# A selective scan and a soft mixture of experts over 16 sequences: four states by TensorE in three sequences, an expert group begun earlier, and a tail in another order

## The chip, the cores and the metric

The kernel is written for one core of a Trainium2 chip. A core has five engines with a queue of instructions each: TensorE (PE) for matrix products, VectorE (DVE), ScalarE (ACT) for functions from tables, GpSimd (POOL), and SyncE (SP), which here only issues DMAs. PSUM takes TensorE's results; the kernel counts it in eight banks, of which a product of 128 x 512 fills one. The metric is device time in microseconds (us) of the whole program. All data are fp32.

## The reference

The input is x of 16 sequences, 512 positions, 256 features. Two layers follow each other, and each adds its input and normalizes. Cut to what matters:

```python
# layer 1: a selective scan in both directions
xf, res = split(x @ in_proj.T)                     # 2 x 512 channels
xf = silu(causal_depthwise_conv(xf))               # again for the backward direction
dt, B, C = split(xf @ x_proj.T)                    # 16, 16 and 16 columns
dt = softplus(dt @ dt_proj.T + b)
dA = dt * A;  dB_u = dt * u * B                    # for each of 16 states
dA_cum = exp(reversed cumsum of shifted dA)
xs = cumsum(dB_u * dA_cum) / (dA_cum + 1e-12)
y = sum over states(xs * C) + u * D                # times silu(res); two directions added
x = layernorm(x + y @ out_proj.T)
# layer 2: soft experts
xn = layernorm(x) * g + b
logits = xn @ slot_embeds_normed                   # 16 experts x 64 slots
dispatch = softmax(logits, over positions)
combine  = softmax(logits, over slots)
slots = dispatch.T @ xn
eo = (gelu(slots @ Wg + bg) * (slots @ Wu + bu)) @ Wd + bd
x = layernorm(x + combine @ eo)
```

## The kernel before

Everything is in one function, `seq_layers`, which goes through the sequences b = 0 to 15. Channels lie on the partitions: 512 channels are four chunks of 128, and a chunk's 512 positions lie along the free axis.

**The scan** (`scan_part`, lines 392 to 470) is the spine. It is called four times for a sequence: for each of the two pairs of chunks (p = 0, 1), forward and then backward (r = 0, 1). Inside, the 16 states are taken in eight pairs n, n+1, and for each pair come the two chunks, so a sequence has 64 chunk steps. In each step POOL multiplies `db = du * bs` (line 427), where `bs` is a row of B broadcast to all partitions by a DMA; ACT makes the decay `exp(dt * A)` (line 444) and a tanh (446); DVE scans along the positions (450 forward, 452 backward) and gates the result, `hg` (455); POOL multiplies by the broadcast row of C, `cs` (456); and TensorE adds the products into an accumulator in PSUM through multiplications by an identity matrix (371).

For two of the 16 states POOL is spared: `DIAG = (5, 13)`, line 31. There `db` is half as long, and TensorE makes the other half: `du` transposed, times a matrix with B's row on its diagonal (`by_diagonal`, line 405), lands as `hd` in a bank of PSUM, and the scan reads it from there. The diagonal matrices lie in DRAM in `diag_dram` (86). They are zeroed once by DMAs on ACT's queue (187 and 188); in `project_unit` a DMA on ACT's queue writes the diagonal's elements, singly (297); and a DMA on SP's queue loads a state's matrices as `dg`, one state pair ahead of its use (420). `dg` has one buffer.

**Work beside the scan.** The rest is cut into pieces by Python generators, which `class Side` (472 to 534) lets in between chunk steps. There are three sides: `prep` prepares the projections of the next part of the scan, `front` finishes a sequence (`finish`, 613: out projection, layer norm, and `dispatch`, 680), and `back` has the experts and the combines. A piece that fills a bank of PSUM yields HOLD, until its result is taken a step later; a generator that waits yields WAIT; GAP asks for a step without a piece. The three sides share the banks that are free (`BANKS`). `begin(steps)` sets the pace: a side's planned pieces are spread over so many chunk steps. A side runs its generators one after another. Within an engine the order of instructions is the order in which this program issues them.

**Layer 2.** `dispatch` makes logits `pl` (687) in eight steps of 128 slots, the softmax over positions `et` on ACT (700), transposes it `pd` (704), and multiplies by the positions `pq` (719); the slots go to DRAM (`s_dram`, 738). `experts(g, lo, hi)` (740) takes two sequences at once, as group g: sequences 2g and 2g+1. It loads weights and slots (`st`, 763), and for each of eight pairs of experts computes `pg` (825, 830), gelu, `pu` (779), and `peo` (806), and writes to `e_dram` (868). `combine(b)` loads these results (`ceo`), makes the softmax over slots (`weights`, 875: logits `cl` 884, exponentials `cm` 898, transposes `ctp` 905), and multiplies: `cpo` (962).

**The main loop** (995 to 1024) adds at each odd b from 3 on the group of experts (b-3)/2 and its two combines to `back`, spread over 128 chunk steps, or 64 in the last sequence. So group 6 (sequences 12 and 13) starts with b = 15. After the last scan comes the **tail** (1025 to 1049), without a scan: `finish(15)` beside `all_weights(14)`, which makes combine weights ahead of time; when both have ended, `experts(7)` beside `all_weights(15)`; when both have ended, the two last combines.

The lines of the main loop and the tail that the change touches:

```python
if b >= 3 and b % 2 == 1:
    g = (b - 3) // 2
    back.add(8 * PAIR, experts(g, 0, 8))
...
back.begin(128 if b % 2 == 1 and b + 1 < nb else 64)
...
back.add(1, all_weights(2 * g, kept))
side_by_side()
front.add(1, experts(g, 0, 8))
back.add(1, all_weights(2 * g + 1, kept))
side_by_side()
```

Of the kernel before, what the change touches and what calls it, by code (L numbers as in the profile page):

```python
# [29 lines left out]
NE = 16  # L30
DIAG = (5, 13)
DIAG_SIZE = P * (P + 1)
# [23 lines left out]
def seq_layers(tc, ident, neghalf, a, out):  # L56
# [22 lines left out]
    with ExitStack() as ctx:  # L79
# [5 lines left out]

        diag_dram = drams.tile([2, len(DIAG), NL, DIAG_SIZE], F32, name="diag_dram")
        const = ctx.enter_context(tc.tile_pool(name="m_const", bufs=1))
# [86 lines left out]

        def constants():
            steps(side[0], "f", "")
            projections(side[1], "b", "_b")
            steps(side[1], "b", "_b")
            outT = const.tile([P, ND, DM], F32, name="outT")
            nc.sync.dma_start(outT, a["out_projT"].rearrange("(c p) o -> p c o", p=P))  # L180
            late(nc.vector.tensor_scalar(outT, outT, 0.5, None, ALU.mult))
            return outT
# [3 lines left out]
        nc.vector.memset(blank, 0.0)  # L186
        for part in diag_dram.rearrange("r i l (p s) -> (r i) p l s", p=P):
            nc.scalar.dma_start(part, blank[:, : NL * (P + 1)].rearrange("p (l s) -> p l s", l=NL))

# [73 lines left out]
        def prep_gate(b, fwd, out):  # L263
# [9 lines left out]
            out["res"] = res  # L273

        def project_unit(b, r, out):

            w = side[r]
            q = f"{b}_{r}"
            yield GAP + 1
            px = bank(f"px_{q}")  # L280
            for c in range(ND):
                nc.tensor.matmul(
                    px[:XW, :], w["xT"][:, c, :], out["u"][:, c, :], start=(c == 0), stop=(c == ND - 1)
                )
            yield HOLD
            xd = p1.tile([XW, L], F32, tag=f"xd_{r}", name=f"xd_{q}")
            bc = dram.tile([2, NS, L], F32, tag="bc", name=f"bc_{q}")
            if r == 0:
                late(nc.scalar.activation(xd, px[:XW, :], AF.Identity, bias=unit))
            else:  # L290

                late(nc.scalar.activation(xd[: XB + NS, :], px[: XB + NS, :], AF.Identity, bias=unit[: XB + NS]))
                nc.scalar.copy(xd[XC:XW, :], px[XC:XW, ::-1])
            nc.sync.dma_start(bc[0], xd[XB : XB + NS, :])
            nc.sync.dma_start(bc[1], xd[XC:XW, :])
            step = DIAG[1] - DIAG[0]
            nc.scalar.dma_start(
                diag_dram[r].rearrange("i l (p s) -> i l p s", p=P)[:, :, :, 0],
                xd[XB + DIAG[0] : XB + NS : step, :].rearrange("i (l p) -> i l p", p=P),
            )  # L300
            out.update(xd=xd, bc=bc)
# [90 lines left out]
        def scan_part(b, r, p, v, accs, done, then):  # L392

            prep.drain()
            prep.gens += [[1, g] for g in [turn_pair(b, r, p, v)] + then]
            w = side[r]
            made = {}
# [12 lines left out]
            for n in range(0, NS, 2):  # L410
                q = f"{b}_{r}_{p}_{n}"
                k = 1 if n + 1 in DIAG else 2

# [3 lines left out]
                nc.sync.dma_start(cs, v["bc"][1, n : n + 2, :].unsqueeze(0).to_broadcast([P, 2, L]))  # L417
                if n + 3 in DIAG:
                    dg = p4.tile([P, L], F32, tag="dg", name=f"dg_{q}", bufs=1)
                    nc.sync.dma_start(  # L420
                        dg.rearrange("p (l s) -> p l s", l=NL),
                        diag_dram[r, DIAG.index(n + 3), :, : P * P].rearrange("l (p s) -> p l s", p=P),
                    )
                for c in chunks:
# [37 lines left out]
                    nxt_n = n if c == chunks[0] else n + 2  # L462
                    if nxt_n + 1 in DIAG:
                        for x in sides:
                            x.take_up()
                        by_diagonal(nxt_n + 1, chunks[1] if c == chunks[0] else chunks[0])
# [146 lines left out]
        def finish(b, y):  # L613
# [64 lines left out]
            yield from dispatch(b, xn, x2T)  # L678

        def dispatch(b, xn, x2T):  # L680

            for sc in range(NSC):
# [30 lines left out]
                if sc % 2 == 1:  # L713
# [14 lines left out]
                    for k in range(NM):  # L728
# [7 lines left out]
                        if k == 0:  # L736
                            late(ins)
                    nc.scalar.dma_start(s_dram[b, :, :, h * 256 : (h + 1) * 256].rearrange("k p s -> p k s"), sl)

        def experts(g, lo, hi):  # L740
# [22 lines left out]
            def load_slots(ep):  # L763
# [6 lines left out]
                return st  # L770

            prefetch()
            st = load_slots(lo)
            yield 0
            def up(e, j, st):
                pu = bank(f"pu_{g}_{e}")
                for fc in range(NF):
                    for k in range(NM):
                        nc.tensor.matmul(  # L779
                            pu[:, fc * P : (fc + 1) * P],  # L780
                            got["Wu", e][:, k, fc * P : (fc + 1) * P],
                            st[:, k, :, j * SL : (j + 1) * SL],
                            start=(k == 0),
                            stop=(k == NM - 1),
                        )
                used[0] += 1
                return pu
# [28 lines left out]
            for ep in range(lo, hi):  # L816
                e0 = 2 * ep
                yield 2
                pgs = []
# [33 lines left out]
                pus = [up(e0 + j, j, st) for j in range(2)]  # L853
                if ep + 1 < hi:
                    st = load_slots(ep + 1)
                bd = p2.tile([P, 2, DM], F32, tag="bd", name=f"bd_{g}_{e0}", bufs=1)
# [10 lines left out]
                late(nc.vector.tensor_tensor(eo.rearrange("p e o -> p (e o)"), po, bd.rearrange("p e o -> p (e o)"), ALU.add))  # L867
                nc.sync.dma_start(e_dram[e0 : e0 + 2, b0 * SL : (b0 + 2) * SL, :].rearrange("e s o -> s e o"), eo)

        def load_x2(b, lc):  # L870
# [57 lines left out]
        def combine(b, kept=None):  # L928

            own = e_dram[:, b * SL : (b + 1) * SL, :].rearrange("(c j) s o -> j s c o", j=2)  # L930
            eos = []
# [13 lines left out]
            nc.sync.dma_start(x1, x1_dram[b].rearrange("(c p) d -> p c d", p=P))  # L945
            x2 = [] if kept else [load_x2(b, 0)]
            yield 0
# [8 lines left out]
            for lc in range(NL):  # L956
                i = f"{b}_{lc}"
                cts, sm = kept.pop((b, lc)) if kept else (yield from weights(b, lc, x2, False))
                yield GAP + 1
# [35 lines left out]
        for b in range(nb):  # L995
            bwd, nxt, accs = {}, {}, {}

            if b >= 3 and b % 2 == 1:
                g = (b - 3) // 2
                back.add(8 * PAIR, experts(g, 0, 8))  # L1000
# [3 lines left out]
            front.begin(64)  # L1004
            back.begin(128 if b % 2 == 1 and b + 1 < nb else 64)

# [34 lines left out]
        g, kept = nb // 2 - 1, {}  # L1041
        back.add(1, all_weights(2 * g, kept))
        side_by_side()
        front.add(1, experts(g, 0, 8))
        back.add(1, all_weights(2 * g + 1, kept))
        side_by_side()
        front.add(1, combine(2 * g, kept))
        back.add(1, combine(2 * g + 1, kept))
        side_by_side()
# [46 lines left out]
```

## Time and profile before

| what | value |
|---|---|
| time, three runs | 5405.57, 5410.14, 5413.56 us (median 5410.14) |
| the profiled execution | 5411.23 us, its span 5409.4 us |
| busy: POOL, DVE, PE, ACT | 87%, 84%, 80%, 76% of the span |
| weight loads of TensorE | 63%, beside its products |
| TensorE's granted clock, mean | 0.889 of full speed |
| DMA | 907.73 MB, 168 GB/s on average |

The costliest groups of instructions on the page, each with its line, engine, operation, output and inputs, shape, count, then busy time and mean ns of one, then the engine's idle time just ahead of them and what ended most of it:

```profile
L456 POOL TENSOR_TENSOR hg<-hg,cs 128x1024 f32<-128x1024 f32 x1024 | 2420.8, 2368 | 128.1 <-DVE hg L455 110.0
L427 POOL TENSOR_TENSOR db<-du,bs 128x1024 f32<-128x1024 f32 (+1 forms) x1024 | 2144.4, 2098 | 232.3 <-DVE h L450 84.7
L371 PE MATMUL acc<-ident,hg 128*128 128x128 f32 x8192 | 1179.3, 295 | 203.3 <-POOL hg L456 181.6
L455 DVE SCALAR_TENSOR_TENSOR hg<-th,h 128x512 f32<-128x512 f32 x1792 | 1185.8, 678 | 177.2 <-PE acc L371 90.4
L452 DVE TENSOR_TENSOR_SCAN h<-h,db 128x512 f32<-128x512 f32 x896 | 1072.8, 1218 | 112.2 <-ACT h L444 107.5
```

POOL's two multiplications make 4565 of its 4732 us. A share of the whole span is a mean over parts with different limits: the page's 40 slices of 135 us show POOL idle in the last two, where the tail has no scan, and TensorE at five or six tenths in the first seven, where there are no experts yet.

```profile
PE   5656666898888978788888977889787897888889
POOL 6999999999999899998999989998999989988600
```

### The profile page before, as it was taken

What the parts mean: (1) busy time and instruction counts of PE and PEld (TensorE: products, weight loads), DVE (VectorE), ACT (ScalarE), POOL (GpSimd) and SP (SyncE); (2) the same over time, 40 slices, a digit from 0 to 9 for tenths busy, and PEclk for the clock granted to TensorE, in tenths of its full rate; (3) what the DMA queues carried; (4) which work ended last, traced back from release to release, by engine and by line L of the source; (5) the groups of instructions that cost most, each with busy time, mean ns of one, the idle gap of its engine ahead of it and who ended that gap; (6) DMA issues with size and microseconds to landing.
All of it is one profiled execution on the core that took longest, in us unless ns stands there. A gap on an engine that the chain in (4) does not pass through costs nothing. (4 is left out here: it accounts for less than half of the span.)

```text
span 5409.4 us, 73721 instructions
## 1 busy us (share of the span) xinstructions
PE 4331.1 (80%) x24144; PEld 3390.0 (63%) x24145; DVE 4559.7 (84%) x6276; ACT 4087.2 (76%) x6515; POOL 4732.1 (87%) x2537
## 2 busy tenths in 40 slices
PE   5656666898888978788888977889787897888889
PEld 3445555676666666677656765667656776667657
DVE  7888988889898899888998888988899889988722
ACT  6677777787888778887877887788788887877641
POOL 6999999999999899998999989998999989988600
PEclk7778778898899988899888989899889998989999
DMA  4334333575446644566446754467444764457436
GB/s 137 131 117 137 125 129 131 189 230 159 156 142 212 225 149 148 158 223 213 131 144 194 232 170 153 132 212 232 149 149 146 225 224 134 145 179 234 126 103 188
DMA packets 595236, 907.73 MB, mean 168 GB/s; under 512 B 78082, under 2 KB 384898, under 8 KB 594852
## 3 DMA queue, kind: packets, MB, share of 16 engines
q1 hardware_dynamic: 521156, 859.87, 49.5%
q10 hardware_dynamic: 73696, 43.14, 2.8%
q8 instruction: 192, 3.15, 0.2%
q14 instruction: 192, 1.57, 0.1%
HBM read 840.86 MB, written 62.01 MB: 167 GB/s over the span
## 5 line engine op out<-in xcount | busy, mean ns | idle before, releaser
L456 POOL TENSOR_TENSOR hg<-hg,cs 128x1024 f32<-128x1024 f32 x1024 | 2420.8, 2368 | 128.1 <-DVE hg L455 110.0
L427 POOL TENSOR_TENSOR db<-du,bs 128x1024 f32<-128x1024 f32 (+1 forms) x1024 | 2144.4, 2098 | 232.3 <-DVE h L450 84.7
L371 PE MATMUL acc<-ident,hg 128*128 128x128 f32 x8192 | 1179.3, 295 | 203.3 <-POOL hg L456 181.6
L455 DVE SCALAR_TENSOR_TENSOR hg<-th,h 128x512 f32<-128x512 f32 x1792 | 1185.8, 678 | 177.2 <-PE acc L371 90.4
L371 PEld LDWEIGHTS acc<-ident,hg 128*128 128x128 f32 x8192 | 1044.9, 154 | 390.8 <-POOL hg L456 240.9
L452 DVE TENSOR_TENSOR_SCAN h<-h,db 128x512 f32<-128x512 f32 x896 | 1072.8, 1218 | 112.2 <-ACT h L444 107.5
L450 DVE TENSOR_TENSOR_SCAN h<-h,db 128x512 f32<-128x512 f32 x896 | 1071.1, 1217 | 48.8 <-ACT h L444 45.7
L446 ACT ACTIVATE th<-rr,Ah_f 128x512 f32<-128x512 f32 x1024 | 725.0, 714 | 186.3 <-DVE hg L455 183.1
L446 ACT ACTIVATE th<-rr,Ah_b 128x512 f32<-128x512 f32 x1024 | 721.5, 712 | 155.2 <-DVE hg L455 147.7
L444 ACT ACTIVATE h<-dt,A_f 128x512 f32<-128x512 f32 x896 | 608.2, 680 | 117.5 <-DVE hg L455 112.6
L444 ACT ACTIVATE h<-dt,A_b 128x512 f32<-128x512 f32 x896 | 608.6, 681 | 108.8 <-DVE hg L455 105.1
L687 PE MATMUL pl<-x2T,seT 128*128 128x512 f32 x512 | 299.1, 715 | 78.7 <-DVE hg L455 37.4
L405 PE MATMUL hd<-dg,duT 128*128 128x128 f32 x2048 | 305.6, 298 | 32.7 <-ACT yt L627 13.5
L830 PEld LDWEIGHTS pg<-st,Wg 128*128 128x128 f32 x2048 | 244.8, 196 | 106.2 <-issue 85.0
L405 PEld LDWEIGHTS hd<-dg,duT 128*128 128x128 f32 x2048 | 283.1, 214 | 38.4 <-ACT yt L627 15.7
L806 PE MATMUL peo<-Wd,ht 128*128 128x256 f32 x1024 | 257.0, 407 | 55.6 <-DVE rr L337 38.6
L779 PE MATMUL pu<-st,Wu 128*128 128x128 f32 x2048 | 254.5, 283 | 50.1 <-DMA Wu<-in_Wu_dram 32.7
L962 PE MATMUL cpo<-ceo,ct 128*128 128x256 f32 x1024 | 254.8, 407 | 46.9 <-DVE rr L337 39.9
L779 PEld LDWEIGHTS pu<-st,Wu 128*128 128x128 f32 x2048 | 244.9, 198 | 61.5 <-DVE h L452 24.2
L830 PE MATMUL pg<-st,Wg 128*128 128x128 f32 x2048 | 269.9, 286 | 4.1 <-DMA Wg<-in_Wg_dram 3.1
L884 PE MATMUL cl<-seT,cx 128*128 128x512 f32 x512 | 244.7, 617 | 32.5 <-DVE res L272 12.3
L806 PEld LDWEIGHTS peo<-Wd,ht 128*128 128x128 f32 x1024 | 205.3, 206 | 97.7 <-DVE rr L337 41.2
(154 smaller groups left out, 6654.8 us busy)
## 6 DMA issues: line engine op xcount, KB each, us to landing
cs<-bc SPq DMA_DIRECT2D x512, 512.0 KB, 3.9
bs<-bc SPq DMA_DIRECT2D x384, 512.0 KB, 5.1
Wg<-in_Wg_dram SPq DMA_DIRECT2D x128, 512.0 KB, 6.0
Wu<-in_Wu_dram SPq DMA_DIRECT2D x128, 512.0 KB, 6.0
Wd<-in_Wd_dram SPq DMA_DIRECT2D x128, 512.0 KB, 5.5
dg<-diag_dram SPq DMA_DIRECT2D x128, 256.0 KB, 4.2
bs<-bc SPq DMA_DIRECT2D x128, 256.0 KB, 3.6
x<-in_x_dram SPq DMA_DIRECT2D x32, 512.0 KB, 6.3
```

The source lines that it names most:

```text
L371: ins = nc.tensor.matmul(accs[c][:, s], hc[:, j, s], ident, is_transpose=True, start=False, stop=(last and j == 1 and lc == NL - 1),)
L405: ins = nc.tensor.matmul(h[:, s], v[c][3][:, s], dg[:, s], start=True, stop=True)
L427: nc.gpsimd.tensor_tensor(db[:, :k, :], du.unsqueeze(1).to_broadcast([P, k, L]), bs[:, :k, :], ALU.mult)
L444: nc.scalar.activation(hs[j][1], dt, AF.Exp, scale=w["A"][:, c, s])
L446: nc.scalar.activation(ths[j], rr, AF.Tanh, bias=LN_1E12 / 2, scale=w["Ah"][:, c, s])
L450: nc.vector.tensor_tensor_scan(h, dec, add, 0.0, ALU.mult, ALU.add)
L452: nc.vector.tensor_tensor_scan(h[:, ::-1], dec[:, ::-1], add[:, ::-1], 0.0, ALU.mult, ALU.add)
L455: nc.vector.scalar_tensor_tensor(hg[:, j, :], th, 1.0, h, ALU.add, ALU.mult)
L456: nc.gpsimd.tensor_tensor(hg, hg, cs, ALU.mult)
L779: nc.tensor.matmul(pu[:, fc * P : (fc + 1) * P], got["Wu", e][:, k, fc * P : (fc + 1) * P], st[:, k, :, j * SL : (j + 1) * SL], start=(k = ...
L806: nc.tensor.matmul(po[:, j * DM : (j + 1) * DM], ht[:, fc, :], got["Wd", e0 + j][:, fc, :], start=(fc == 0), stop=(fc == NF - 1),)
L830: nc.tensor.matmul(pg[:, fc * P : (fc + 1) * P], got["Wg", e][:, k, fc * P : (fc + 1) * P], st[:, k, :, j * SL : (j + 1) * SL], start=Fals ...
```

## The change

In sequences 0 to 2 four states instead of two go by TensorE: 3, 7, 11 and 15. The later sequences keep 5 and 13. `diag_dram` has room for four, and the zeroing DMAs are double in number; those of the backward direction are issued with `constants()`.

Group 6 of the experts is added to `back` at b = 14 instead of 15, behind what is left of group 5, and the pace of sequence 14 is set for 100 steps.

In the tail, `experts(7)` starts on one side while `finish(15)` with its dispatch runs on the other: a pair of experts waits (`ready`) until the slots it needs have been written, and its slots are loaded when they are. Behind `finish(15)` the front side makes the combine weights of 14 and 15 and combines 15; the other side combines 14 after the experts. `combine` waits for its experts and for each of the kept weights.

```diff
-DIAG = (5, 13)
+DIAGS = 4
...
-        diag_dram = drams.tile([2, len(DIAG), NL, DIAG_SIZE], F32, name="diag_dram")
+        diag_dram = drams.tile([2, DIAGS, NL, DIAG_SIZE], F32, name="diag_dram")
...
         def constants():
+            blanks(1)
...
-        for part in diag_dram.rearrange("r i l (p s) -> (r i) p l s", p=P):
-            nc.scalar.dma_start(part, blank[:, : NL * (P + 1)].rearrange("p (l s) -> p l s", l=NL))
+
+        def blanks(r):
+            for part in diag_dram[r].rearrange("i l (p s) -> i p l s", p=P):
+                nc.scalar.dma_start(part, blank[:, : NL * (P + 1)].rearrange("p (l s) -> p l s", l=NL))
+
+        blanks(0)
...
+        def diag_of(b):
+
+            return (3, 7, 11, 15) if b < 3 else (5, 13)
...
-            step = DIAG[1] - DIAG[0]
+            ds = diag_of(b)
             nc.scalar.dma_start(
-                diag_dram[r].rearrange("i l (p s) -> i l p s", p=P)[:, :, :, 0],
-                xd[XB + DIAG[0] : XB + NS : step, :].rearrange("i (l p) -> i l p", p=P),
+                diag_dram[r, : len(ds)].rearrange("i l (p s) -> i l p s", p=P)[:, :, :, 0],
+                xd[XB + ds[0] : XB + NS : ds[1] - ds[0], :].rearrange("i (l p) -> i l p", p=P),
             )
...
-            w = side[r]
+            w, ds = side[r], diag_of(b)
...
-                k = 1 if n + 1 in DIAG else 2
+                k = 1 if n + 1 in ds else 2
...
-                if n + 3 in DIAG:
+                if n + 3 in ds:
...
-                    if nxt_n + 1 in DIAG:
+                    if nxt_n + 1 in ds:
...
+        dispatched = {}
+        expert_done = set()
+
         def dispatch(b, xn, x2T):
...
                     nc.scalar.dma_start(s_dram[b, :, :, h * 256 : (h + 1) * 256].rearrange("k p s -> p k s"), sl)
+                    dispatched[b] = h + 1
...
+            def ready(ep):
+                return dispatched.get(b0 + 1, 0) > ep // 2
+
             prefetch()
-            st = load_slots(lo)
+            st = None
             yield 0
...
                 e0 = 2 * ep
+                while not ready(ep):
+                    yield WAIT
+                if st is None:
+                    st = load_slots(ep)
+                    yield WAIT
                 yield 2
...
-                if ep + 1 < hi:
-                    st = load_slots(ep + 1)
+                st = load_slots(ep + 1) if ep + 1 < hi and ready(ep + 1) else None
...
+            expert_done.add(g)
...
         def combine(b, kept=None):
 
+            while b // 2 not in expert_done:
+                yield WAIT
...
-                cts, sm = kept.pop((b, lc)) if kept else (yield from weights(b, lc, x2, False))
+                while kept is not None and (b, lc) not in kept:
+                    yield WAIT
+                cts, sm = (yield from weights(b, lc, x2, False)) if kept is None else kept.pop((b, lc))
...
-            if b >= 3 and b % 2 == 1:
-                g = (b - 3) // 2
+
+            if 3 <= b < nb - 1 and b % 2 == 1 or b == nb - 2:
+                g = (b - 2) // 2
                 back.add(8 * PAIR, experts(g, 0, 8))
...
-            back.begin(128 if b % 2 == 1 and b + 1 < nb else 64)
+            back.begin(128 if b % 2 == 1 and b + 1 < nb else 100 if b == nb - 2 else 64)
...
         g, kept = nb // 2 - 1, {}
-        back.add(1, all_weights(2 * g, kept))
-        side_by_side()
-        front.add(1, experts(g, 0, 8))
-        back.add(1, all_weights(2 * g + 1, kept))
-        side_by_side()
-        front.add(1, combine(2 * g, kept))
-        back.add(1, combine(2 * g + 1, kept))
+        back.add(1, experts(g, 0, 8))
+        for b in (2 * g, 2 * g + 1):
+            front.add(1, all_weights(b, kept))
+        back.add(1, combine(2 * g, kept))
+        front.add(1, combine(2 * g + 1, kept))
         side_by_side()
```

More of the change, by code (lines that the diff above doesn't have):

```diff
@@ L421, in scan_part @@
                         dg.rearrange("p (l s) -> p l s", l=NL),
-                        diag_dram[r, DIAG.index(n + 3), :, : P * P].rearrange("l (p s) -> p l s", p=P),
+                        diag_dram[r, ds.index(n + 3), :, : P * P].rearrange("l (p s) -> p l s", p=P),
                     )
@@ L945, in combine @@
             nc.sync.dma_start(x1, x1_dram[b].rearrange("(c p) d -> p c d", p=P))
-            x2 = [] if kept else [load_x2(b, 0)]
+            x2 = [load_x2(b, 0)] if kept is None else []
             yield 0
```

## The prediction

> **What bounds the kernel now.** I read the page first (busy shares: POOL 87%, DVE 84%, PE 80%), then cut the span at every 64th `db` multiplication of line 427, of which each sequence has exactly 64. That gives stages with different limits: sequences 0 to 2 take 295, 299 and 300 us, later ones with an expert group 324 to 333 us, those with combines 306 us, the last 371 us, and a tail without scans 292 us. The table of windows for the stages the change touches (us, then busy us of PE, PEld, DVE, ACT, POOL, TensorE's granted clock, DMA share, GB/s):
>
> ```profile
> 41.00:336.00 295.00, 169.89 (x847) 132.26 (x847) 258.92 (x305) 208.70 (x321) 285.45 (x147) 0.72 0.39 128
> 336.00:635.00 299.00, 199.79 (x1037) 157.42 (x1037) 263.63 (x324) 227.40 (x362) 292.70 (x154) 0.80 0.40 129
> 635.00:935.00 300.00, 204.42 (x1044) 160.18 (x1044) 262.20 (x322) 226.62 (x361) 292.34 (x153) 0.78 0.39 128
> 4441.00:4746.00 305.00, 243.96 (x1299) 186.16 (x1298) 279.67 (x382) 243.15 (x404) 292.19 (x155) 0.89 0.45 143
> 4746.00:5117.00 371.00, 315.09 (x1840) 253.09 (x1838) 290.68 (x425) 269.62 (x424) 294.80 (x156) 0.92 0.59 189
> 5117.00:5409.00 292.00, 260.04 (x1313) 193.68 (x1311) 77.77 (x207) 87.38 (x172) 24.38 (x50) 0.97 0.45 140
> ```
>
> Sequences 0 to 2 are bound by POOL (97 to 98% busy) with PE a third idle. In the last sequence no engine is full and PE is nearest. The tail is PE's: 260 of 292. POOL's two forms of `db`, from the groups kept apart by form:
>
> ```profile
> L427 POOL TENSOR_TENSOR db<-du,bs 128x1024 f32<-128x1024 f32 x768 | 1816.5, 2370 | 175.4 <-issue 66.3 <-DVE h L450 57.2 <-DVE h L452 42.2
> L427 POOL TENSOR_TENSOR db<-du,bs 128x512 f32<-128x512 f32 x256 | 327.9, 1281 | 57.0 <-DVE h L450 27.5 <-DVE h L452 15.0 <-POOL hg L456 11.4
> ```
>
> A state taken to TensorE saves POOL 2.370 - 1.281 = 1.09 us per chunk. At the head, ACT's and SP's timelines show two waits that matter:
>
> ```profile
> 2.22 5.90 ACTq L188 DMA_DIRECT2D diag_dram<-blank  x4
> 8.15 1.28 ACT L230 ACT_TABLE_LOAD   x1 [8.15 <-DMA diag_dram<-blank]
> ...
> 46.81 0.37 SPq L420 DMA_DIRECT2D dg<-diag_dram  x1
> ```
>
> Four blanking DMAs hold ACT until 8.1; the first `dg` load leaves SP only at 46.81, 11.8 us after the diagonal's write of 1024 single elements was issued (34.97). In the tail, PE's timeline has its gaps in brackets:
>
> ```profile
> 5177.22 2.16 PE L687 MATMUL pl<-x2T,seT 128*128 128x512 f32 x4
> 5182.84 1.12 PE L704 MATMUL pd<-ident,et 128*128 128x128 f32 x4 [3.46 <-ACT et L700]
> ...
> 5223.70 1.11 PE L704 MATMUL pd<-ident,et 128*128 128x128 f32 x4 [2.55 <-ACT et L700]
> ...
> 5230.04 1.11 PE L704 MATMUL pd<-ident,et 128*128 128x128 f32 x4 [2.55 <-ACT et L700]
> ...
> 5377.41 25.80 PE L962 MATMUL cpo<-ceo,ct 128*128 128x256 f32 x112 [4.63 <-DMA ceo<-e_dram]
> ```
>
> PE waits on the softmax chain while sequence 15 is dispatched, and on the experts' output before the last combine.
>
> **The Trainium skill.** "GPSIMD Engine Reference", Elementwise side-by-side cycle accounting, gives a POOL tensor_tensor of 2048 fp32 columns as 4497 ns, by elements; the trace's 2370 and 1281 ns for 1024 and 512 agree. "ScalarE: Activation LUTs", What ACT_TABLE_LOAD costs: about 1283 ns; the trace has 1283. "DMA: Bandwidth & Descriptors", Rules for kernel authors: a non-contiguous last dimension becomes one descriptor for each element; the 11.8 us above is consistent with that. "PSUM - Partial Sum Buffer", Engine vs sequencer instructions, calls ACT's queue strict FIFO; the table load at 8.15, held by DMA issues ahead of it, agrees.
>
> **Part 1, four states in sequences 0 to 2.** Two more states, two directions, four chunks: 16 halved `db`, 16 x 1.09 = 17.4 us of POOL a sequence. Added beside it: 16 `hd` products of 8 matmul records on PE (1.06 us each, 17 us, where 100 are free), 8 more `dg` loads of 256 KB, matched by 8 `bs` loads halved from 512 KB, and `dec` exps of 0.71 for 0.68 us on ACT. DVE does the same work. POOL's need in sequence 1 falls from 292.7 to 275.3 us; DVE's stays at 263.6. POOL now idles 6 us where DVE is 88% full; in sequence 14, where DVE is 92% full, it idles 13. After the change DVE is at 92%, so I take POOL at 96%: 275.3/0.96 = 287, a gain of 12 to 13 us. Sequence 2: the same. Sequence 0: 15, before its head.
>
> What the head adds: the order of instructions on ACT has all eight blanking DMAs before the first table load, four more than now. They go out in turn as earlier ones land (the fourth now waits from 4.0 to 7.8). I take 4 us for ACT's first copy, bounds 2.5 and 7; from there to the scan everything hangs on that copy. [...] The diagonal's first write has 2048 elements, and its `dg` now precedes the `bs` and `cs` of the second pair in SP's queue. If landing doubles, that pair's `bs` comes some 10 us later, but DVE's first results hold POOL until 51.45 anyway, so I take 1 us, bounds 0 and 8. Later diagonal writes come 40 us ahead of their use: nothing.
>
> With one `dg` buffer each load waits for the previous state's two products. SP's order puts the load for state 11 behind `bs` 14, so after POOL's `db` of pair 8. From there POOL has five `hg` of 2.37 and 7 us of `db`, 19 us, before it needs pair 10's `hg`; load 4.2, product 1.1 and DVE 4 need about 10. Covered, but DVE already waits 106 us in all for `hd` (76.4 + 30.0, 81 times), now inside its slack. Sum of part 1: 15 + 12.5 + 12.5 - 4 - 1 = 35 us, bounds 15 and 52.
>
> **Part 2, the group begun a sequence sooner.** By the code group 6 joins at sequence 14. The order of TensorE's instructions says otherwise. `back` runs its generators in turn; the combines of group 5 fill sequence 14 (last `cpo` after chunk step 58 of 64, before: 62), and only `pg_0`, `pg_1` of group 6 get in, after step 63. In sequence 15 the last `peo` comes after step 39 instead of 40, and the combines behind it follow at the same steps (43 to 60). The 371 us stay: gain 0, bounds -6 and +6. Sequences 3 to 12 have identical orders on TensorE.
>
> **Part 3, the tail.** Its start up to `pl_0` at 5177.2 is unchanged. From there PE's pure work is eight expert pairs of 13.1 (5302.03 to 5315.13), 104.8; eight weight steps of 4.31, 34.5; eight `cpo` of 3.45, 27.6; dispatch (8 `pl` of 1.72, 8 `pd` of 0.5, 4 `pq` of 3.46), 31.6: 198.5 us, against 226.0 until PE's last matmul at 5403.2. So 27.5 us are gaps (18.4 in brackets) and slow restarts after them. In the new order the expert pairs lie between the later dispatch steps, the weights of 14 between expert pairs, and the weights of 15 between the last `peo` and the last combine. Still open are the first softmax (3.5), the second (2.55), the copy before `pq_1` (0.6), `pd_2` (1.5), and `st_0`: `pq_1` to data is 1.1 + 2.1 + 5.1 = 8.3 us (now 5198.5 to 5206.9) with 5 us of PE work to lie under, 3.4. With 1 us for `st_1`, 12.6; restarts 1 to 2. So 13 us come off. ACT gets nine more table loads, 11.5 us, but is busy 87 of 292: hidden, except where a load stands in the softmax chain. Weight loads now ride over 140 us instead of 118, so DMA eases. I take 14 us, bounds 4 and 22.
>
> **Sum.** 35 + 0 + 14 = 49 us off the profiled run's 5411.2 (span 5409.4), which lies 1.1 us above the median: 5410 - 49 = **5361 us**.
>
> **Rivals.** *A: POOL's relief isn't cashed.* DVE's chain (exp, scan, gate) becomes the limit in sequences 0 to 2 and PSUM banks held by `hd` delay the side work. For it: DVE at 88% already and waits for `hd`; against: sequence 14 runs with DVE at 92% and POOL at 96%. Gain there 5 less the head's 5, so the tail alone: 5396. *B: slower, by the single `dg` buffer.* These sequences have 48 `dg` loads, each serving two chunks. If every load reaches DVE late, and the lateness goes on to POOL, each costs its delay; from 1.25 us a load (60 us) the 35 + 14 + 11 are gone and the kernel is slower by over 0.2%; at 2 us, 96: 5457. Against: the 9 us margin above. *C: the move does what it says.* Part of group 6 fits in sequence 14, and the pair costs 330 + 315 instead of 306 + 371, 32 less: 5329. Against: the instruction order. *D: the tail's new order stalls PE* as often as the old one (`pg` waits for `st` ahead of `pd` in PE's queue): 5375.
>
> **How the numbers follow.** Forecast 0.60, A 0.15, D 0.14, C 0.05, B 0.06. The forecast's own range is 5361 - 23 to 5361 + 21; with A's and D's the 8-in-10 range is 5335 to 5393. A measurement of this kernel tells 0.2% (11 us) from no change: faster 0.92 (all but B and a poor A), same 0.03, slower 0.05.
>
> **What would show it.** Right: 768 - 48 = 720 full and 256 + 48 = 304 half forms of `db`; sequences 1 and 2 at 285 to 289 us with POOL near 275 busy; ACT's first table load at 11 to 15; sequence 15 still near 371 with `pg` of group 6 starting at its edge; a tail of about 278. Wrong: `hd` waits on DVE followed by idle POOL, sequence 15 much shorter, or PE gaps before `pg` in the dispatch.

## The result, and the profile after

| | median of four | lowest to highest |
|---|---|---|
| before | 5411.73 us | 5405.57 to 5413.56 |
| after | 5351.97 us | 5346.47 to 5358.26 |

The ratio is 0.9892, with a 95% interval from 0.9875 to 0.9909: the kernel is faster by 1.1%, 60 us where 49 were forecast. The profiled execution took 5353.58 us, its span is 5351.8, against 5409.4. Cut at every 64th `db` as before, and behind the last one at its end, the two spans differ like this:

| stage | before | after | difference | forecast |
|---|---|---|---|---|
| start to the first `db` | 40.7 | 46.1 | +5.4 | +5 |
| sequence 0 | 295.4 | 274.9 | -20.5 | -15 |
| sequence 1 | 298.8 | 283.6 | -15.2 | -12.5 |
| sequence 2 | 300.3 | 283.5 | -16.8 | -12.5 |
| sequences 3 to 13 | 3505.3 | 3499.1 | -6.2 | 0 |
| sequence 14 | 305.6 | 316.7 | +11.1 | 0 |
| sequence 15 to the end of its last `db` | 368.9 | 371.9 | +3.0 | 0 |
| tail | 294.4 | 275.9 | -18.5 | -14 |

The windows of the changed stages (us, then busy us of PE, PEld, DVE, ACT, POOL, the granted clock, DMA share, GB/s):

```profile
46.10:321.00 274.90, 179.37 (x973) 145.82 (x972) 254.42 (x304) 207.60 (x321) 268.48 (x147) 0.77 0.44 136
321.00:604.60 283.60, 203.23 (x1159) 164.91 (x1160) 260.96 (x322) 224.92 (x359) 275.63 (x154) 0.83 0.44 137
604.60:888.10 283.50, 203.69 (x1176) 165.50 (x1175) 261.70 (x323) 226.87 (x362) 275.68 (x154) 0.83 0.43 135
4387.20:4704.00 316.80, 251.03 (x1339) 189.76 (x1337) 284.32 (x392) 244.99 (x409) 295.02 (x158) 0.91 0.45 140
4704.00:5075.90 371.90, 309.41 (x1811) 248.72 (x1810) 283.77 (x417) 259.51 (x412) 291.00 (x152) 0.91 0.59 187
5075.90:5351.80 275.90, 254.35 (x1314) 192.81 (x1312) 79.50 (x209) 99.85 (x182) 25.68 (x52) 0.97 0.48 148
```

In sequences 1 and 2 POOL is still the limit: it is busy 275.6 of 283.6 us, 97%, with DVE at 92%. Sequence 14 has become 11 us longer, while PE's busy time rose by 6 and DVE's by 4, so waiting was added there; PE's share comes with 34 more records (1339 against 1305), most of them pieces of a combine that before came later. In the tail the time without TensorE fell from 32.4 to 21.5 us, and TensorE's busy time from 262.0 to 254.4: `pl` took 659 ns on average and now 596, `pd` 335 and now 278. The granted clock is hardly a rival: in the tail it was 0.97 both times, sequence 14 grew longer at 0.91 than it was at 0.89, and in sequences 1 and 2, where it rose from 0.80 and 0.78 to 0.83, it is POOL's busy time that shrank. The two forms of `db`, kept apart by form on POOL:

```profile
L436 POOL TENSOR_TENSOR db<-du,bs 128x1024 f32<-128x1024 f32 x720 | 1703.0, 2370 | 167.0 <-issue 75.8 <-DVE h L461 43.9 <-DVE h L459 39.0
L436 POOL TENSOR_TENSOR db<-du,bs 128x512 f32<-128x512 f32 x304 | 389.3, 1281 | 58.7 <-DVE h L459 39.2 <-POOL hg L465 9.2 <-DMA bs<-bc 4.1
```

48 full forms have become halves, at unchanged durations. The head on ACT's timeline:

```profile
2.22 9.81 ACTq L191 DMA_DIRECT2D diag_dram<-blank  x8
12.07 1.28 ACT L235 ACT_TABLE_LOAD   x1 [12.07 <-DMA diag_dram<-blank]
```

The first table load comes 3.9 us later. In the tail, the lines of PE's timeline with more than half a microsecond of waiting, with `pl_0`, the bias products of `pg_0` and the last product:

```profile
5138.48 2.16 PE L699 MATMUL pl<-x2T,seT 128*128 128x512 f32 x4
5140.56 1.98 PE L847 MATMUL pg<-ident,bg_rows 64*128 64x512 f32 x4
5144.09 0.66 PE L716 MATMUL pd<-ident,et 128*128 128x128 f32 x4 [1.54 <-ACT et L712]
...
5149.02 0.66 PE L716 MATMUL pd<-ident,et 128*128 128x128 f32 x4 [2.55 <-ACT et L712]
5150.35 5.30 PE L731 MATMUL pq<-dis,xn 128*128 128x256 f32 x16 [0.67 <-ACT dis L721]
...
5159.91 0.66 PE L716 MATMUL pd<-ident,et 128*128 128x128 f32 x4 [0.83 <-ACT et L712]
5161.27 0.68 PE L852 MATMUL pg<-st,Wg 128*128 128x128 f32 x4 [0.70 <-DMA st<-s_dram]
...
5331.54 13.98 PE L988 MATMUL cpo<-ceo,ct 128*128 128x256 f32 x64
```

After 5161.3 no wait of PE is in brackets again. From `pl_0` to its last product it takes 207.0 us (5138.48 to 5345.52) where it took 226.0.

### The profile page after: what moved, and what is told of

Read it like the earlier page. It is cut to its first block, busy times and chain, and to the rows that moved or that the text cites. A ratio compares the mean times of both kernels' runs of the same rounds, so it can differ in the third digit from the quotient of the medians.

```text
span 5351.8 us, 74548 instructions
## 1 busy us (share of the span) xinstructions
PE 4331.0 (81%) x24529; PEld 3407.3 (64%) x24529; DVE 4551.7 (85%) x6276; ACT 4089.7 (76%) x6518; POOL 4680.8 (87%) x2537
## 5 line engine op out<-in xcount | busy, mean ns | idle before, releaser
L436 POOL TENSOR_TENSOR db<-du,bs 128x1024 f32<-128x1024 f32 (+1 forms) x1024 | 2092.1, 2047 | 225.7 <-issue 78.6
L464 DVE SCALAR_TENSOR_TENSOR hg<-th,h 128x512 f32<-128x512 f32 x1744 | 1158.5, 681 | 185.3 <-PE acc L380 112.1
L380 PE MATMUL acc<-ident,hg 128*128 128x128 f32 x8192 | 1157.9, 291 | 111.1 <-POOL hg L465 88.5
L380 PEld LDWEIGHTS acc<-ident,hg 128*128 128x128 f32 x8192 | 1029.6, 152 | 290.3 <-POOL hg L465 129.1
L461 DVE TENSOR_TENSOR_SCAN h<-h,db 128x512 f32<-128x512 f32 x872 | 1044.9, 1221 | 105.0 <-ACT h L453 95.4
L459 DVE TENSOR_TENSOR_SCAN h<-h,db 128x512 f32<-128x512 f32 x872 | 1045.7, 1221 | 47.7 <-ACT h L453 46.1
L453 ACT ACTIVATE h<-dt,A_f 128x512 f32<-128x512 f32 x872 | 591.5, 680 | 104.8 <-DVE hg L464 101.7
L453 ACT ACTIVATE h<-dt,A_b 128x512 f32<-128x512 f32 x872 | 592.3, 680 | 88.3 <-DVE hg L464 84.8
L414 PE MATMUL hd<-dg,duT 128*128 128x128 f32 x2432 | 371.1, 302 | 83.1 <-ACT duT L364 27.1
L414 PEld LDWEIGHTS hd<-dg,duT 128*128 128x128 f32 x2432 | 342.6, 217 | 94.4 <-ACT duT L364 28.9
L699 PE MATMUL pl<-x2T,seT 128*128 128x512 f32 x512 | 285.3, 685 | 72.0 <-DVE hg L464 32.4
L796 PE MATMUL pu<-st,Wu 128*128 128x128 f32 x2048 | 258.2, 286 | 52.9 <-DMA Wu<-in_Wu_dram 24.2
```

The lines of the kernel that those rows point to most:

```text
L380: ins = nc.tensor.matmul(accs[c][:, s], hc[:, j, s], ident, is_transpose=True, start=False, stop=(last and j == 1 and lc == NL - 1),)
L414: ins = nc.tensor.matmul(h[:, s], v[c][3][:, s], dg[:, s], start=True, stop=True)
L436: nc.gpsimd.tensor_tensor(db[:, :k, :], du.unsqueeze(1).to_broadcast([P, k, L]), bs[:, :k, :], ALU.mult)
L453: nc.scalar.activation(hs[j][1], dt, AF.Exp, scale=w["A"][:, c, s])
L459: nc.vector.tensor_tensor_scan(h, dec, add, 0.0, ALU.mult, ALU.add)
L461: nc.vector.tensor_tensor_scan(h[:, ::-1], dec[:, ::-1], add[:, ::-1], 0.0, ALU.mult, ALU.add)
```

## The experiments

Each ratio is to runs of the kernel before on the same chip, with its 95% interval. The stage lengths are from each run's own profile.

### The parts alone

Four states in sequences 0 to 2 on the kernel before, main loop and tail untouched:

```diff
-DIAG = (5, 13)
+DIAGS = 4
...
+            return (3, 7, 11, 15) if b < 3 else (5, 13)
```

> The four states alone, on the kernel before: main loop and tail as they were. Theory (the stages add up as the changed kernel's own stages show: head +5.4, sequences 0 to 2 20.5, 15.2 and 16.8 shorter): fourth sequence begins near 888, all later sequences and the tail as before, total 5411 - 47 = 5364 us. Rival (the early sequences and the late ones act on one another, through the granted clock or the DMA): the later stages move by more than 3 us in sum and the total lies at 5376, the 35 us forecast, or above.

Measured: ratio 0.9918 (0.9903 to 0.9933), some 44 us. The first `db` at 47.2, sequences 0 to 2 at 274.9, 283.0 and 283.4, sequence 3 begins at 888.6: the theory's stages. The sign that the rival named is there too: in this profile, whose 5376.48 us are the longest of its four runs, all that comes behind sequence 2 is 11.6 us longer than before, among it sequence 15 with 375.7 us and the tail with 298.2, with the same code and the same order on TensorE as before. Sequence 15 takes 375.0 to 375.9 us in four other profiles with that order, so this may be scatter; for the tail of before there are only two profiles, and it stays open. The whole, 44 us, lies nearer to the theory's 47 than to the rival's 35.

The new tail alone, with two states everywhere and group 6 at sequence 15:

```diff
-            return (3, 7, 11, 15) if b < 3 else (5, 13)
+            return (5, 13)
...
-            if 3 <= b < nb - 1 and b % 2 == 1 or b == nb - 2:
-                g = (b - 2) // 2
+            if b >= 3 and b % 2 == 1:
+                g = (b - 3) // 2
...
```

> The new tail alone on the kernel before: two states by TensorE everywhere, group 6 at sequence 15, paces of before. Theory (the tail's gain is its own and adds to the others): tail from the last db 275 to 277 us instead of 294, ratio to before 0.9965, that is 18 to 19 us. Rival (part of the gain belongs to what runs ahead of the tail in the changed kernel): tail at 285 or more, ratio 0.998 or above.

Measured: ratio 0.9958 (0.9943 to 0.9973), that is 23 us, with an interval from 15 to 31 that holds the 18 to 19 expected, and a tail of 276.9 us, as the theory said. The tail's gain is its own.

### The group begun sooner

The changed kernel with group 6 and the paces of before, four states and new tail kept:

```diff
-            if 3 <= b < nb - 1 and b % 2 == 1 or b == nb - 2:
-                g = (b - 2) // 2
+            if b >= 3 and b % 2 == 1:
+                g = (b - 3) // 2
...
-            back.begin(128 if b % 2 == 1 and b + 1 < nb else 100 if b == nb - 2 else 64)
+            back.begin(128 if b % 2 == 1 and b + 1 < nb else 64)
```

> The changed kernel with group 6 put back to sequence 15 and the paces of before; four states and the new tail stay. Theory (the earlier start costs time, since the higher pace in sequence 14 lays pieces of the combines of sequence 11 where their waits hold the scan's products in TensorE's queue): sequence 14 back from 316.7 to 305 to 307 us, sequence 15 at 369, total 5352 - 14 = 5338 us, faster than both kernels. Rival (the longer sequence 14 comes from the granted clock or from what went ahead of it): sequence 14 stays at 314 or more and the total at 5350 to 5354.

Measured: median 5346.28 us, ratio 0.9869 (0.9854 to 0.9883). Sequence 14 is back at 307.0, as the theory said; the whole time lies between the theory's 5338 and the rival's 5350. The ratio is worth 71 us (63 to 79), and the two parts alone, 44 and 23, add up to 67: they add without a sign of acting on one another. And the changed kernel with one number, the pace, changed:

```diff
-            back.begin(128 if b % 2 == 1 and b + 1 < nb else 100 if b == nb - 2 else 64)
+            back.begin(128 if b % 2 == 1 and b + 1 < nb else 192 if b == nb - 2 else 64)
```

> The changed kernel with one number changed: the pace of sequence 14 set for 192 steps instead of 100, so that its credit per step is about what it was before; group 6 is still added there. Theory (pace): sequence 14 at 305 to 308, total 5337 to 5343. Rival (adding the group itself costs: its weights' loads, its first slots, its bank held at the edge): sequence 14 at 312 or more, total 5348 to 5354.

Measured: median 5351.38 us, ratio 0.9881 (0.9865 to 0.9898). The median lies in the rival's range, the interval reaches into the theory's, and the profiled execution, 5342.05 us, was the fastest of its four runs, so the whole time can't tell the two apart; sequence 14 lies between them at 311.4. The steps tell more. This is the time from each fourth `db` to the next in sequence 14, us:

```
before       18.6 19.6 19.0 20.6 21.2 18.2 18.5 18.8 18.6 19.1 21.5 17.6 18.6 16.4 21.6 17.6
after        19.1 20.0 19.3 20.9 19.7 24.2 18.6 18.8 18.6 20.8 18.5 14.1 20.9 14.0 27.8 21.3
no_sooner    19.1 20.1 19.0 20.6 21.2 18.2 18.6 18.8 18.6 19.4 21.5 17.9 18.6 16.4 21.3 17.6
sooner_slow  19.1 20.0 19.0 20.7 21.2 18.2 18.5 18.8 18.6 19.4 21.5 17.9 18.6 16.4 21.2 22.1
```

At the slower pace the first sixty steps are those of no_sooner, and the two places that stick out in after (24.2 and 27.8) are gone, though the group is still added in sequence 14. So the pace made them. The last four steps stay long (22.1 against 17.6), and that goes with the added group and not with the pace: of the 10 us of sequence 14 some 5 are the pace's and some 4 the group's. Sequence 15 was 3.6 us shorter in this profile (367.8 against 371.4, the pair 679.2 against 678.4), but that is within its scatter, given below.

What happens at the first place is in the timelines of POOL, ACT, PE and DVE of the changed kernel, in order of time, with the lines between them left out:

```profile
4495.30 0.24 POOL L611 TENSOR_SCALAR m_sh<-m_sh 128x4 f32<-128x4 f32 x1
4495.57 2.08 ACT L616 ACTIVATE x<-x,m_sh,m_rs 128x256 f32<-128x256 f32 x4 [4.20 <-POOL m_sh L611]
4499.34 0.51 ACT L668 ACTIVATE xn<-x,m_r 128x256 f32<-128x256 f32 x1 [1.69 <-POOL m_r L660]
4499.76 0.67 ACT L920 ACTIVATE cm<-cl,cnm 128x512 f32<-128x512 f32 x1
4500.57 2.08 PE L414 MATMUL hd<-dg,duT 128*128 128x128 f32 x8 [5.36 <-ACT cm L920]
4501.22 0.15 DVE L940 TENSOR_REDUCE csm<-csm 128x1 f32<-128x2 f32 x1 [5.85 <-ACT cm L920]
4502.68 1.23 DVE L461 TENSOR_TENSOR_SCAN hd<-dec,hd 128x512 f32<-128x512 f32 x1 [1.11 <-PE hd L414]
```

ACT waits twice for POOL's small layer norm instructions of `finish`, 4.20 and 1.69 us. Behind them in its queue stands `cm`, the exponential that reads a combine's logits out of their PSUM bank. Two things hang on it. By the releaser that the trace names, the scan's product `hd` waits 5.36 us for that reading. And DVE itself waits 5.85 us for `cm`, since the sum `csm` of the combine stands ahead of the scan in its queue; only 1.11 us behind that are a wait for `hd`. So the bank that `hd` needs is not what held the scan alone: DVE would have stood for the late `cm` without it. PE's timelines show what the pace has moved: in the changed kernel a combine's product comes ahead of the out projection `po`,

```profile
4471.27 3.62 PE L988 MATMUL cpo<-ceo,ct 128*128 128x256 f32 x16
...
4481.07 5.41 PE L642 MATMUL po<-outT,yt 128*128 128x256 f32 x16 [4.44 <-DVE cx L997]
```

and in no_sooner, whose sequence 14 begins 2 us earlier, they are the other way round (in sooner_slow too, at 4470.67 and 4481.07):

```profile
4470.27 3.62 PE L642 MATMUL po<-outT,yt 128*128 128x256 f32 x16
...
4480.66 3.62 PE L988 MATMUL cpo<-ceo,ct 128*128 128x256 f32 x16
...
4486.76 1.06 PE L414 MATMUL hd<-dg,duT 128*128 128x128 f32 x8
```

There the layer norm behind `po` is through POOL by 4487.5 instead of 4499.3, ACT waits 0.78 and 0.63 us for it, no `cm` stands behind it, and `hd` waits for nothing. So the new wait comes with a swap of two pieces of the same work, made by the credit, the part of a piece that a side may lay at each chunk step. The second place (27.8) was read less closely: there ACT's queue has a silu of 2048 columns with two table loads, 4.5 us, ahead of the softmax that TensorE waits for. In no_sooner the same silu and two loads stand at 4655.28, with the scan's own exponential behind them, so what they cost at this place isn't shown.

Because the times lay close, both kernels ran again side by side:

> The changed kernel itself once more, beside no_sooner_again on one chip, so that the price of the earlier start has a comparison of its own. Theory (the earlier start costs 10 us or more in sequence 14): this lies 9 to 15 us above no_sooner_again, sequence 14 at 316 to 318. Rival (the first profile's sequence 14 was one slow execution): sequence 14 at 305 to 308 and the two kernels within 5 us.

> The changed kernel with group 6 at sequence 15 again, the other half of that comparison: theory 9 to 15 us under after_again, rival within 5 us of it.

Measured: 5350.56 (5348.80 to 5356.53) against 5345.69 (5343.30 to 5350.39), ratios to before 0.9883 (0.9866 to 0.9899) and 0.9871 (0.9856 to 0.9886). Sequence 14 took 316.9 and 306.8: its 10 us repeat to 0.2. So sequence 14 is the theory's, but the medians are only 4.9 us apart, within the rival's 5. Sequence 15 blurs the rest: 371.9 and 368.4 with the group begun sooner, and between 368.9 and 375.9 in the eight profiles here that have sequences 14 and 15 in the order of before. The pair of sequences averages 687.0 us over two profiles against 680.4 over eight: a net price of some 7 us, of which only the 10 in sequence 14 are certain.

### More states by TensorE

The four kernels from here on are made from no_sooner: their edits come on top of its own.

If POOL sets these sequences, more states should help further. First in the same sequences: six states, 5, 7, 9, 11, 13 and 15, one in each of six state pairs in a row.

```diff
-            return (3, 7, 11, 15) if b < 3 else (5, 13)
+            return (5, 7, 9, 11, 13, 15) if b < 3 else (5, 13)
```

> As no_sooner, with six states by TensorE (5, 7, 9, 11, 13, 15) in the first three sequences, so that a dg load follows each of five state pairs in turn through the single buffer. Twelve zeroing DMAs instead of eight: head 4 us later. Theory (POOL alone sets these sequences until DVE does): POOL's need falls from 275.6 to 258, DVE's 262 is the floor, sequences 1 and 2 at 268 to 273 instead of 283. Rival (the single dg buffer: the load leaves after the second product of the state before and has one chunk step of 3.65 us to cover 4.1 of load and 1.1 of product): each of 20 loads a sequence late by 1 to 3 us, sequences 1 and 2 at 285 to 310.

Measured: ratio 1.0042 (1.0026 to 1.0058), slower than before. The first `db` comes at 53.7 us, and sequences 1 and 2 take 310.9 and 322.3 us, more than even the rival's 285 to 310. The groups of `hd` in sequence 2, first in the changed kernel (DVE's scans that read it, then PE's products):

```profile
L461 DVE TENSOR_TENSOR_SCAN hd<-dec,hd 128x512 f32<-128x512 f32 x16 | 19.4, 1216 | 1.5 <-ACT th L455 1.3 <-PE hd L414 0.2
L459 DVE TENSOR_TENSOR_SCAN hd<-dec,hd 128x512 f32<-128x512 f32 x16 | 19.4, 1215 | 0.4 <-PE hd L414 0.4
```

```profile
L414 PE MATMUL hd<-dg,duT 128*128 128x128 f32 x256 | 40.7, 310 | 17.9 <-ACT duT L364 8.7 <-issue 4.0 <-DMA dg<-diag_dram 3.9
```

and with six states:

```profile
L461 DVE TENSOR_TENSOR_SCAN hd<-dec,hd 128x512 f32<-128x512 f32 x24 | 29.3, 1221 | 10.2 <-PE hd L414 10.2
L459 DVE TENSOR_TENSOR_SCAN hd<-dec,hd 128x512 f32<-128x512 f32 x24 | 29.2, 1217 | 11.3 <-PE hd L414 11.3
```

```profile
L414 PE MATMUL hd<-dg,duT 128*128 128x128 f32 x384 | 59.3, 304 | 44.2 <-DMA dg<-diag_dram 33.2 <-DVE rr L346 5.9 <-DVE hg L464 3.1
```

PE waits 33.2 us of the sequence for `dg`, DVE 21.5 for `hd`, and POOL, whose busy time fell to 259.1 as computed, idles the rest. The waits start where the buffer comes free, as here (PE and SP, lines between them left out):

```profile
714.76 1.06 PE L414 MATMUL hd<-dg,duT 128*128 128x128 f32 x8
715.85 0.39 SPq L429 DMA_DIRECT2D dg<-diag_dram  x1
724.40 2.04 PE L414 MATMUL hd<-dg,duT 128*128 128x128 f32 x8 [7.27 <-DMA dg<-diag_dram]
```

The load leaves SP 0.03 us after the end of the last product of the state before. So do 13 of the 24 loads of sequence 2; with four states 2 of 16, the others 0.6 us or more after it. This is rival B of the prediction, alive: with six states in a row the single `dg` buffer is what the loads wait for. With four, spaced by a free pair, DVE waits 0.6 us for `hd` in the whole sequence. Six states have both closer and more loads, and no run parts the two. A second `dg` buffer wasn't tried.

Then four states in the even sequences 4 to 14 too, which carry combines:

```diff
-            return (3, 7, 11, 15) if b < 3 else (5, 13)
+            return (3, 7, 11, 15) if b < 3 or b % 2 == 0 else (5, 13)
```

> As no_sooner, with the four states in sequences 4, 6, 8, 10, 12 and 14 too (those that carry combines and take 305.6 us, POOL 292 of them, DVE 280, PE 244). Theory (POOL sets those sequences as well, and DVE can run at 97%): POOL's need falls by 16 times 1.09 us to 275, DVE's 280 is the floor, 286 to 292 each, total 5346 - 6 x 16 = 5250 us, range 5235 to 5270. Rival (work beside the scan sets them: PE's pieces, the banks that hd takes from them, DVE near full): 300 to 306 each, total 5315 to 5350.

Measured: ratio 1.0122 (1.0102 to 1.0141), slower than either theory allowed. The even sequences take 312 to 320 us instead of 306, the odd ones 339 to 343 instead of 328 to 330, the tail 303 instead of 275. In sequence 4, POOL's busy time did fall, from 292.8 to 277.9. The groups of PE there, without the change (no_sooner):

```profile
L988 PE MATMUL cpo<-ceo,ct 128*128 128x256 f32 x112 | 28.3, 411 | 6.4 <-DVE rr L346 6.4
...
L414 PE MATMUL hd<-dg,duT 128*128 128x128 f32 x128 | 19.0, 297 | 2.3 <-ACT yt L636 2.3
```

and with it:

```profile
L414 PE MATMUL hd<-dg,duT 128*128 128x128 f32 x248 | 43.3, 331 | 28.0 <-ACT dis L721 7.1 <-DVE hg L464 4.9 <-ACT duT L364 4.4
...
L988 PE MATMUL cpo<-ceo,ct 128*128 128x256 f32 x87 | 19.8, 379 | 0.0
```

The counts are the message: 25 fewer records of `cpo` fall into the sequence (and 8 fewer each of `cl`, `ctp` and `pl`, a whole piece), and what doesn't fit makes the next one, and in the end the tail, longer. PE's waits ahead of `hd` rose from 2.3 to 28.0 us: `hd` meets the work beside the scan in TensorE's queue. But DVE waited no longer for `hd` than without the change (5.2 us against 5.8), so these waits do not reach the scan through `hd` itself. The code also counts `hd` among the three banks that the work beside the scan shares, which would keep its pieces out; that is an inference, and what weighs most wasn't separated. It has the shape of rival A, in sequences that are full of other work; in sequences 0 to 2 there is room.

### The head

The zeroing DMAs, in pairs behind each chunk's tap instead of all eight ahead of ACT's first copy:

```diff
-        blanks(0)
...
                 if b == 0:
+                    blanks(c)
                     late(nc.scalar.activation(xf[:, c, :], xf[:, c, :], AF.Silu))
```

> As no_sooner, and the eight zeroing DMAs issued on ACT's queue in pairs, each pair between a chunk's tap and its silu, instead of all ahead of the first copy. Theory (the head hangs on ACT's first copy): that copy at 7 instead of 13.4, first db of the scan at 39 to 41 instead of 46, total 5 to 7 under no_sooner, 5332. Rival (the waits of these DMAs only move to the later place in ACT's queue, and the pieces of the head behind them come as late): first db at 45 to 50, total 5338 to 5342.

Measured: ratio 0.9871 (0.9856 to 0.9885), where no_sooner has 0.9869. ACT's first copy did come at 6.12 instead of 13.4, and `du` was ready at 39. But POOL's first `db` waited:

```profile
36.47 2.52 POOL L346 TENSOR_TENSOR du<-dt,xf 128x512 f32<-128x512 f32 x2 [34.42 <-ACT dt L327]
46.15 7.09 POOL L434 TENSOR_TENSOR db<-du,bs 128x1024 f32<-128x1024 f32 x4 [7.16 <-DMA bs<-bc]
```

and SP's queue shows why its `bs` is late:

```profile
35.70 0.37 SPq L771 DMA_DIRECT2D Wg<-in_Wg_dram  x1
36.18 0.45 SPq L301 DMA_DIRECT2D bc<-xd  x1
36.68 0.42 SPq L302 DMA_DIRECT2D bc<-xd  x1
41.61 0.38 SPq L427 DMA_DIRECT2D dg<-diag_dram  x1
42.09 0.45 SPq L423 DMA_DIRECT2D bs<-bc  x1
```

`xd` ended at 33.2, but `bc` stood behind a weight load, and `bs` behind the `dg` that waits for the diagonal. Both out of the way, by a zero tile in another buffer and the rows of two state pairs issued ahead of the first `dg`:

```diff
-        blank = p2.tile([P, 4 * DM], F32, tag="W", name="blank", bufs=3)
+        blank = p4.tile([P, 2, L], F32, tag="hg", name="blank", bufs=4).rearrange("p j l -> p (j l)")
...
+                if b == r == p == n == 0:
+                    load_rows(2)
```

> As blank_late (zeroing in pairs behind the first copies), with the zero tile taken from a buffer that no early load needs, and the first dg load issued behind the bs and cs of the first two state pairs. Theory (in blank_late the head's 6 us were lost in SP's queue: bc behind a weight load that waited for the zero tile's buffer, bs behind the dg that waited for the diagonal): first db at 38 to 40, total 6 to 8 under no_sooner, ratio 0.9855 against its 0.9869. Rival (the row loads come late for another reason, the DMA engines' load by zeroing): first db at 44 to 47, ratio as no_sooner's.

Measured: ratio 0.9868 (0.9851 to 0.9884). The first `db` is at 43.8, still waiting for `bs`, and sequence 3 begins at 884.5 instead of 886.1. Closer to the rival: 1.6 us by the profile, nothing by the times. The 5 us of the head's start are not lost at one place; when ACT is freed, the row loads are next.

## Why the prediction was right, and where not

The sign, the range and the order of the parts were right; the sum was 11 us short. That it came so near is in part luck: by the two profiles part 1 brought 12.1 us and part 3 4.5 us more than forecast, sequences 14 and 15 lost 14.1 where nothing was forecast, and 6.2 came in sequences 3 to 13, which the change was not meant to touch. The misses cancel in part.

**Part 1, size.** The forecast was 35 us, and 47.1 came. The mechanism holds: POOL's busy time in sequence 1 fell by 17.0 us, computed 17.4; DVE's stayed (263.5 and 261.0). The mis-sized term is POOL's share: 96% was taken from sequence 14, and it was 97.2%, hardly lower than before. 275.3 at 97.2% would have been 283 instead of 287. Sequence 14 was the wrong pattern; that its side work meets the scan and that of the early sequences doesn't is the likely reason, not a shown one. Sequence 0 gained 20.5 us, 3 more than POOL's relief of 17.4, as POOL's idle time there fell from 9.6 to 6.4.

The head's sum was right, 5.4 us against 5, and its first term too, 3.9 us for the first copy against 4. The second term was not what was measured. The 1 us stood for the `bs` of the second state pair, and POOL did wait for it, in the changed kernel's sequence 0:

```profile
46.11 4.70 POOL L436 TENSOR_TENSOR db<-du,bs 128x1024 f32<-128x1024 f32 x2 [0.32 <-DMA bs<-bc]
54.96 2.50 POOL L436 TENSOR_TENSOR db<-du,bs 128x512 f32<-128x512 f32 x2 [4.15 <-DMA bs<-bc]
```

These 4.15 us stand where before POOL waited 3.79 us for DVE's first results (at 51.45), as the prediction argued, so they cost little. The 1.5 us that came behind the first copy lie ahead of the first `db`. The 9 us of margin around the single `dg` buffer were enough: PE waited 3.9 us for `dg` in sequence 2, but DVE only 0.6 for `hd`.

**Part 2, wrong sign in one stage.** The prediction saw that the combines of group 5 would end earlier (the last `cpo` after step 58 instead of 62) and that group 6 would do hardly anything in sequence 14, and put the rest at nothing. It didn't ask what the moved pieces would now stand beside. To put this at nothing is the step that failed: no_sooner shows that the earlier start costs 10 us in sequence 14, and sooner_slow that about half of it is the pace. At one place the traces show how, a late exponential in ACT's queue that DVE and `hd` wait for; the rest was not followed up. Net of sequence 15 it is about 7, at the edge of the 6 that were allowed. Rival C fell for the reason that was held against it: `back` runs its generators in turn, and the last `cpo` of group 5 stands at 4701.7, 2 us before the end of sequence 14. The first `pg` of group 6 came at 4731.5, in sequence 15; in no_sooner at 4736.8. Slots were there earlier: the four `pq` of sequence 13's dispatch came at 4580.0, 4623.5, 4679.4 and 4723.6, and by the code the first two pairs of experts wait only for the first of them.

**Part 3, size.** 13 us were to come off between `pl_0` and the last product, and 19.0 did. The mis-sized terms are the gaps left: 3.5 for the first softmax became 1.54, since the bias products of `pg_0` (1.98 us) lie in it, which need no slots; `st_0` cost 0.70 instead of 3.4; the five gaps over half a microsecond add up to 6.3 instead of 12.6. Rival D fell.

**Not forecast.** Sequences 3 to 13 are 6.2 us shorter, with the same order on TensorE. In nine other profiles with two states there that stretch takes 3497 to 3510 us, and single sequences jump by 2 to 3 us from run to run. Only sequence 3 sets the kernels apart: it takes 322.3 to 323.3 us in the nine profiles with four states ahead of it, 324.1 and 328.3 in the two with two states. So some 2 us may belong to the change, for a reason that stays open; the rest is not put down to it.

The version without the earlier start lies at 5346 us in both its measurements (ratios 0.9869 and 0.9871). It is faster than before; that it is faster than the changed kernel is shown for sequence 14, and for the whole time it is likely but within the scatter.

## What to carry to other kernels

A piece of work moved to another step costs what it meets there: look up which instruction of the critical engine will stand behind it, and whose queue its buffer waits in, even where no work is added. Relief of a full engine is worth its full size only where the other queues have room: 17 us of POOL brought 15 to 17 in sequences 1 and 2, and a relief of 15 us in sequence 4 came with a longer sequence. With a single buffer for loads, look at the distance between its uses before their number: with a free pair between them DVE waited 0.6 us in a sequence, with uses in pair after pair 21.5.

## What the runs showed of the hardware

A load that follows a write of single elements came late. In the kernel with six states a diagonal write of 3072 elements was issued at 713.03 and a `dg` load at 715.85; the product that needs it began at 724.40, 8.5 us later, where the page of the changed kernel has 4.1 us as the median for a `dg` load. Sequences 1 and 2 have four such loads, 2.7 to 2.8 us behind such a write; their products began 8.0, 6.9, 8.5 and 5.9 us after the load's issue. Where PE waited for one of the other `dg` loads there, it was 2.9 to 5.9 us. No run takes the write away, so that the write is the cause stays argued.
